# VectorE's dependent chains planned in parts, with VectorE's order left to the compiler

## The chip, the cores and the metric

The kernel runs on one core of one Trainium2 chip. The metric is device time in microseconds (us), the median over runs of one launch. "TensorE" and "PE" are the same engine, as are VectorE and DVE, ScalarE and ACT, GpSimd and POOL, SyncE and SP.

## What is computed

32 images of 128 channels and 56 x 56 points pass through two layers. Cut to what matters:

```python
# layer 0: convolution of signs
x = x + conv3x3(sign(groupnorm(x)), sign(w)) * Alpha
# layer 1: each point is a token of 128 channels
t = to_tokens(x)                                  # 3136 tokens per image
n = layernorm(t); q, k, v = n@Wq+bq, n@Wk+bk, n@Wv+bv
t = t + q * sum(k * v, over tokens)               # linear attention
n = layernorm(t)
p, e = top2(softmax(n @ router_w + router_b))     # 8 experts, 2 per token
t = t + sum_j p_j/sum(p) * (n @ expert_w[e_j] + expert_b[e_j])
out = from_tokens(t)
```

## The kernel before

The kernel is one long straight program, a software pipeline over the 32 images. An image's tokens stand in 25 chunks of up to 128 tokens (the last has 64), and these in 7 blocks of four. Each image goes through these steps, each of them a small Python function that emits the instructions of one engine: sums for the group norm (ScalarE), signs (ScalarE), convolution (`conv`, PE, 9 matmuls per 8 rows), adding it to x (`conv_add`, VectorE), transposing to tokens (`to_tokens`, PE), statistics of the first layer norm (`stats`, `var1`, `rstd1`, VectorE), the Gram matrix (`scaled`, `gram`), the product kv (`kv_1` to `kv_8`, taking turns on PE and VectorE), the bias of q (`bias`, VectorE), the projection (`project`, `project_out`, `project_add`), the second norm (`var2`, `rstd2`) and the routing (`route_1` to `route_5`, nearly all VectorE).

The experts are computed in two ways. The first 8 or 12 chunks of an image, and all chunks of the last four images, are "dense": gates are transposed, stored to memory, read back spread over all partitions (`spread`, a DMA to the tile `bc`), multiplied with the tokens (`gated`, VectorE, 128 x 1024) and put through all eight experts (`experts`, PE, tile `ff`). The other chunks of the first 28 images are "sorted": tokens are numbered by their pair of experts (`pair_of`, `places`, `row_numbers`, `row_scalars`), scattered to memory by GpSimd (tile `rows`), and, when a group of 8 or 4 images is complete, a list of tiles is made (`list_1`, `list_2`) and each tile of 128 rows goes through just two experts (`tile_load`, `tile_turn`, `tile_experts`, `tile_read`, `tile_sum`, `tile_out`). The results are gathered back (`result_rows`, `gather`).

What sets the order is a planner written in the kernel. `at(...)` (L444) records a step: its due time, engine, estimated work in us, function, the steps it comes after, and the buffers it takes and frees. `in_order` (L104) is a list scheduler: it keeps a clock for each engine, and of the steps that could start within `AHEAD` = 0.3 us of the earliest one, it takes that with the earliest due time (`urgency`, L133; a step that empties a PSUM bank counts as 7 us more urgent). A step that follows one of another engine is ready 0.5 or 0.8 us (`HOP`) after it. The list that results is emitted under `tc.manual_schedule(engines=IN_ORDER)` (L1684): the engines in `IN_ORDER` (L72: PE, VectorE, ScalarE) run exactly in the emitted order. The others, GpSimd and SyncE's DMA queue, are ordered by the compiler, which goes by the emitted order as a preference and by its own estimate of what is ready. In either case the order is fixed when the program starts, each engine takes its instructions strictly one after the other, and semaphores make it wait for its inputs.

A step of several VectorE instructions is one unit of this list; its instructions stand side by side on the engine, as in `rstd_of` (L464), where each needs the one before:

```python
for _ in range(NEWTON):
    nc.vector.tensor_mul(square, dst, dst)
    nc.vector.scalar_tensor_tensor(square, square, -0.5, var, ALU.mult, ALU.mult)
    nc.vector.scalar_tensor_tensor(dst, square, 1.5, dst, ALU.add, ALU.mult)
```

Lines that the prediction speaks of: L458 to L461 variance, L468 to L480 reciprocal root, L580 `conv_add`, L688 to L690 `kv_2`, L695 the matmul of `kv_3`, L736 `bias`, L862 to L893 routing, L1057 `gated`, L1075 `experts`, L1158 and L1159 `pair_of`, L1186 the first matmul of `places`, L1587 and L1592 `tile_sum` and `tile_out`.

Of the kernel before, what the change touches and what calls it, by code (L numbers as in the profile page):

```python
# [71 lines left out]
IN_ORDER = {mybir.EngineType.PE, mybir.EngineType.DVE, mybir.EngineType.Activation}  # L72
# [12 lines left out]
AHEAD = 0.3  # L85
# [7 lines left out]
class Step:  # L93
# [3 lines left out]
    def __init__(self, due, key, engine, work, do, args, after, take, free, delay, slack):  # L97
        self.due, self.key, self.engine, self.work = due, key, engine, work
        self.do, self.args, self.delay, self.slack = do, args, delay, slack
        self.after, self.take, self.free = after, take, free  # L100
        self.done = None


def in_order(steps):  # L104
# [28 lines left out]
    def urgency(s):  # L133

        return s.due - (EMPTIES if any(r in BANKS for r, _ in s.free) else 0.0)

    order = []
    while len(order) < len(steps):
        best = None
        for engine, pool in waiting.items():  # L140
# [9 lines left out]
            ((t, s) for t, s in starts if t <= first + AHEAD), key=lambda e: (urgency(e[1]), e[0])  # L150
# [7 lines left out]
        for f in followers.get(s.key, []):  # L158
            missing[f.key] -= 1

            same = f.engine == s.engine and (not s.delay or f.key[0] == s.key[0])
            f.ready = max(f.ready, clock[s.engine] if same else s.done + s.slack + HOP[f.engine])
            if not missing[f.key]:
                waiting.setdefault(f.engine, []).append(f)
# [4 lines left out]
def conv_attn_moe_kernel(  # L169
# [173 lines left out]
    def prepare():  # L343
# [3 lines left out]
        inv_c = spool.tile([1, C], F32, tag="kv", bufs=1, name="inv_c")  # L347
# [96 lines left out]
    def at(due, key, engine, work, do, *args, after=(), take=(), free=(), delay=0.0, slack=0.0):  # L444
        steps[key] = Step(due, key, engine, work, do, args, after, take, free, delay, slack)
# [6 lines left out]
    def var_of(stats, name):  # L452
# [3 lines left out]
        diff = spool.tile([C, n_ck], F32, tag="diff", name="diff")  # L456
        var = spool.tile([C, n_ck], F32, tag=name, name=name)
        nc.vector.tensor_sub(diff, mean_e, mean_o)  # L458
        nc.vector.scalar_tensor_tensor(diff, diff, 0.25, diff, ALU.mult, ALU.mult)
        nc.vector.scalar_tensor_tensor(var, m2_e, C * LN_EPS, m2_o, ALU.add, ALU.add)  # L460
        nc.vector.scalar_tensor_tensor(var, var, 1.0 / C, diff, ALU.mult, ALU.add)  # L461
        return var

    def rstd_of(var, dst):  # L464

        square = spool.tile([C, n_ck], F32, tag="square", bufs=1, name="square")
# [6 lines left out]
        )  # L473
        nc.vector.tensor_tensor(
            dst.bitcast(I32), guess.to_broadcast(shape), square.bitcast(I32), ALU.subtract
        )
        for _ in range(NEWTON):
            nc.vector.tensor_mul(square, dst, dst)
            nc.vector.scalar_tensor_tensor(square, square, -0.5, var, ALU.mult, ALU.mult)
            nc.vector.scalar_tensor_tensor(dst, square, 1.5, dst, ALU.add, ALU.mult)  # L480
# [8 lines left out]
    def plan_image(i: int):  # L489
# [57 lines left out]
        for j in range(GN_PARTS):  # L547
# [7 lines left out]
            s - 25, ("gn_total", i), "DVE", 0.09, gn_total,  # L555
# [4 lines left out]
            s - 23, ("gn_neg", i), "DVE", 0.08, gn_neg,  # L560
# [45 lines left out]
        def stats(g, st):  # L606
            for c in blocks[g]:
                n = rows_of(c)
                nc.vector.bn_stats(st[:n, c, :], d["tok"][:n, c, :C])  # L609

        def var1():
            d["var1"] = var_of(st1, "var1")
            d["r1"] = spool.tile([C, n_ck], F32, tag="r1", name=f"r1_{i}")

        def rstd1():
            rstd_of(d["var1"], d["r1"])
# [12 lines left out]
        for g in range(n_blk):  # L629
# [13 lines left out]
                due + 2, ("stats1", i, g), "DVE", 0.78 * share, stats, g, st1,  # L643
# [3 lines left out]
            s + 43, ("var1", i), "DVE", 0.45, var1,  # L647
            after=[("stats1", i, g) for g in range(n_blk)]
            + [("project_out", i - 2, 8), ("rstd1", i - 2)],
        )  # L650
        at(s + 44, ("rstd1", i), "DVE", 1.25, rstd1, after=[("var1", i)])
# [33 lines left out]
        def kv_2():  # L685
            tok_sum = d["g_sb"][:, C : C + 1]
            prod = spool.tile([C, C], F32, tag="prod", bufs=1, name=f"prod_{i}")
            nc.vector.scalar_tensor_tensor(prod, bv_bc, tok_sum, d["gv"], ALU.mult, ALU.add)  # L688
            nc.vector.tensor_mul(prod, prod, wk_sb)
            nc.vector.scalar_tensor_tensor(prod, wv_bk, tok_sum, prod, ALU.mult, ALU.add)  # L690
# [6 lines left out]
        def kv_4():  # L697

            kv = spool.tile([C, C], F32, tag="kv", bufs=1, name=f"kv_{i}")
            nc.vector.tensor_add(kv, n_bkbv, d["kv_ps"])  # L700
            nc.vector.tensor_mul(move[:, :C], wq_sb, kv)
# [8 lines left out]
        def kv_6():  # L710
# [3 lines left out]
            nc.vector.scalar_tensor_tensor(kr[:, 0, :], rw_sb, d["kvc"], one, ALU.mult, ALU.mult)  # L714
            nc.vector.scalar_tensor_tensor(
# [22 lines left out]
        for g in range(n_blk):  # L738
# [15 lines left out]
            ("PE", 0.25, kv_1), ("DVE", 0.73, kv_2), ("PE", 0.25, kv_3), ("DVE", 0.62, kv_4),  # L754
            ("PE", 0.25, kv_5), ("DVE", 0.28, kv_6), ("PE", 0.46, kv_7), ("ACT", 0.15, kv_8),
# [49 lines left out]
        def project_add(j):  # L805
# [10 lines left out]
            for c in cs:  # L816
                nc.vector.bn_stats(st2[:n, c, :], d["tok"][:n, c, :C])  # L817

        for j, cs in enumerate(q_groups):
# [12 lines left out]
                s + 87 + 3.5 * j, ("project_add", i, j), "DVE", 1.18 * share, project_add, j,  # L832
# [8 lines left out]
        def var2():  # L841
            d["var2"] = var_of(st2, "var2")
            d["r2"] = spool.tile([C, n_ck], F32, tag="r2", name=f"r2_{i}")

        def rstd2():
            rstd_of(d["var2"], d["r2"])
# [13 lines left out]
        def largest(vals, suffix):  # L860
            top, hot, best = narrow(f"top{suffix}"), wide(f"hot{suffix}"), narrow(f"best{suffix}")
            nc.vector.tensor_reduce(top, vals, AX.X, ALU.max)  # L862
            nc.vector.tensor_tensor(hot, vals, over_e(top), ALU.is_equal)
            nc.vector.tensor_tensor(hot, hot, over_c(rank), ALU.mult)
            nc.vector.tensor_reduce(best, hot, AX.X, ALU.max)
            nc.vector.tensor_tensor(hot, hot, over_e(best), ALU.is_equal)
            return top, hot, best

        def route_1():
            logit = wide("logit")  # L870
            nc.vector.tensor_tensor(logit, lgp, over_c(d["cq"]), ALU.add)
            nc.vector.tensor_tensor(logit, logit, over_e(d["r2"]), ALU.mult)
            nc.vector.tensor_tensor(logit, logit, over_c(rb_bc), ALU.add)
            d["logit"] = logit

        def route_2():
            d["top1"], d["hot1"], d["best1"] = largest(d["logit"], "1")
            rest = wide("rest")
            nc.vector.scalar_tensor_tensor(
                rest.rearrange("p c e -> p (c e)"),  # L880
                d["hot1"].rearrange("p c e -> p (c e)"),
                -BIG,
                d["logit"].rearrange("p c e -> p (c e)"),
                ALU.mult,
                ALU.add,
            )
            d["rest"] = rest

        def route_3():
            d["top2"], d["hot2"], d["best2"] = largest(d["rest"], "2")  # L890
# [7 lines left out]
        def route_5():  # L898
            gate1, gate2 = narrow("gate1"), narrow("gate2")
            nc.vector.tensor_tensor(gate1, d["ratio"], ones[:, :n_ck], ALU.add)  # L900
            nc.vector.reciprocal(gate1, gate1)
            nc.vector.tensor_mul(gate2, d["ratio"], gate1)
# [3 lines left out]
        def dense_gates():  # L906
# [7 lines left out]
            nc.vector.tensor_tensor(hot2, hot2, bc(d["gate2"]), ALU.mult)  # L914

            full = n // PER
            for lo, hi, per in ((0, full, PER), (full, n_db, n - full * PER)):
# [11 lines left out]
                nc.vector.tensor_tensor(plain, first, second, ALU.add)  # L929
                nc.vector.tensor_tensor(scaled_by, plain, r2, ALU.mult)  # L930
# [31 lines left out]
        def gate_parts():  # L962
# [5 lines left out]
            nc.vector.tensor_sub(parts[:, :, 1, :], p, parts[:, :, 0, :])  # L968
            nc.vector.tensor_sub(parts[:, :, 2, :], rem, parts[:, :, 1, :])

        def parts_store():
# [15 lines left out]
            s + 118, ("var2", i), "DVE", 0.45, var2,  # L987
            after=[("project_add", i, j) for j in range(last_q + 1)]
            + [("dense_gates", i - 2), ("row_scalars", i - 2)],
        )  # L990
        at(s + 119, ("rstd2", i), "DVE", 1.25, rstd2, after=[("var2", i)])
        at(s + 125, ("route_1", i), "DVE", 0.85, route_1, after=[("rstd2", i)] + routed)
        at(s + 126, ("route_2", i), "DVE", 1.7, route_2, after=[("route_1", i)])
        at(s + 128, ("route_3", i), "DVE", 1.53, route_3, after=[("route_2", i)])
        at(s + 130, ("route_4", i), "ACT", 0.14, route_4, after=[("route_3", i)])
        at(s + 131, ("route_5", i), "DVE", 0.43, route_5, after=[("route_4", i)])
        at(
            s + 135, ("dense_gates", i), "DVE", 0.8 * heavy, dense_gates,
# [16 lines left out]
            s + 138, ("gate_parts", i), "DVE", 0.65 * heavy, gate_parts,  # L1015
# [136 lines left out]
        def pair_of():  # L1152
# [6 lines left out]
            nc.vector.tensor_tensor(low, best1, best2, ALU.min)  # L1159

            nc.vector.scalar_tensor_tensor(pair, high, -3.0, high, ALU.add, ALU.mult)
            nc.vector.scalar_tensor_tensor(pair, pair, 0.5, low, ALU.mult, ALU.add)
            d["pair"] = pair

            mark = spool.tile([C, n_sort], F32, tag="mark", bufs=1, name=f"mark_{i}")
            nc.vector.tensor_add(mark, pair, no_row[:, most - n_sort :])
            shape = [C, n_sort, N_PAIR]
# [5 lines left out]
            )  # L1173
            with nc.allow_low_precision(reason="numbers up to four"):
# [42 lines left out]
        def row_numbers():  # L1217
# [3 lines left out]
            nc.vector.tensor_tensor(own, hot[:, :n_sort, :], d.pop("places")[:, :n_sort, :], ALU.mult)  # L1221
            nc.vector.tensor_reduce(place, own, AX.X, ALU.add)
            d["row_no"] = spool.tile([C, n_sort], U32, tag="row_no", bufs=4, name=f"row_no_{i}")
# [5 lines left out]
        def row_scalars():  # L1229
# [6 lines left out]
            swap, move_by, g = tmp("swap"), tmp("move_by"), tmp("g")  # L1236
# [498 lines left out]
```

## Time and profile before

| | |
|---|---|
| time, median of 3 runs | 2410.17 us (2406.23 to 2425.59) |
| the profiled execution's own time | 2401.99 us |
| its span, first to last instruction | 2400.3 us |
| granted TensorE clock, mean | 0.966 |
| PE busy | 2144.5 us (89%), 12074 instructions |
| weight loads (beside PE) | 1454.5 us (61%) |
| VectorE busy | 2097.1 us (87%), 6360 instructions |
| ScalarE busy | 1530.2 us (64%), 4883 instructions |
| GpSimd busy | 972.5 us (41%), 971 instructions |
| DMA | 448.56 MB, 187 GB/s in the mean |

An engine's busy time is the union of its instructions' intervals. On VectorE the interval of an instruction can overlap that of the next by some 80 ns, so the start of one to the start of the next is what an instruction costs. The profile's view of waits gives, for each line, the idle time of its engine just before it and who ended it; waits of 35 ns between two instructions of VectorE are not in it. VectorE's costliest groups: `gated` 449.1 us (384 instructions, 1177 ns each), the two lots of statistics 169.4 and 183.0 us (800 each), `conv_add` 151.2 us (224), `project_add`'s first addition 139.8 us (256 whole ones, 546 ns each).

### The profile page before, as it was taken

The numbers are of one execution on the slowest core, as the hardware profiler recorded it, in microseconds if no ns is written. First come the engines' busy times: TensorE is split into PE (matmuls) and PEld (weight loads), VectorE is DVE, ScalarE is ACT, GpSimd is POOL, SyncE is SP. The second block draws the span as 40 slices with busy tenths as digits, with TensorE's granted clock in tenths as the row PEclk, the third lists the DMA queues.
The fourth block names the chain that finished last, engine by engine and source line by source line (L and its number), as shares of the span: only waits on it lengthen the run. The fifth ranks groups of instructions, "written<-read, shape, count | busy, mean of one in ns | idle before, by whom it ended". The sixth has DMA issues, their size and how long they took to land. (4 is left out here: it accounts for less than half of the span.)

```text
span 2400.3 us, 45146 instructions
## 1 busy us (share of the span) xinstructions
PE 2144.5 (89%) x12074; PEld 1454.5 (61%) x12074; DVE 2097.1 (87%) x6360; ACT 1530.2 (64%) x4883; POOL 972.5 (41%) x971
## 2 busy tenths in 40 slices
PE   4889888888899999888999999898999888999889
PEld 2555555555676776555766766555676655766534
DVE  3899999999999999998889889999898777788875
ACT  3756666656788888566778876555687755674311
POOL 1033333333223234544445534554444444433554
PEclk9999999999999999999999999999999989999999
DMA  4044444445555655455667666666577656878688
GB/s 161 28 144 142 143 134 135 174 122 165 165 157 171 187 182 174 151 185 193 190 217 239 200 196 195 204 200 215 191 214 226 211 163 207 256 225 251 192 258 313
DMA packets 317740, 448.56 MB, mean 187 GB/s; under 512 B 61065, under 2 KB 223153, under 8 KB 317490
## 3 DMA queue, kind: packets, MB, share of 16 engines
q1 hardware_dynamic: 289090, 386.97, 51.4%
q0 software_dynamic: 27392, 55.17, 7.7%
q10 hardware_dynamic: 1008, 3.54, 0.4%
q8 instruction: 102, 1.67, 0.3%
q14 instruction: 148, 1.21, 0.2%
HBM read 319.51 MB, written 126.00 MB: 186 GB/s over the span
## 5 line engine op out<-in xcount | busy, mean ns | idle before, releaser
L1268 POOL DMA_INDIRECT rows<-tok,row_no x428 | 487.3, 1139 | 893.0 <-ACT tok L1262 400.0
L1075 PE MATMUL ff<-gated,ew_d 128*128 128x512 f32 (+1 forms) x1536 | 737.5, 608 | 78.8 <-DVE gated L1057 62.1
L1338 POOL DMA_INDIRECT back<-res,res_no x428 | 475.8, 1112 | 520.1 <-PE back_ps L1353 201.0
L1057 DVE TENSOR_TENSOR gated<-tt,bc 128x1024 f32<-128x1024 f32 x384 | 449.1, 1177 | 67.4 <-PE ff L1075 41.3
L1075 PEld LDWEIGHTS ff<-gated,ew_d 128*128 128x128 f32 x1536 | 277.0, 196 | 324.4 <-issue 220.6
L569 PE MATMUL cv<-xs,w_bin 128*128 128x448 bf16 x2016 | 438.6, 365 | 11.8 <-ACT xs L535 5.8
L1575 ACT ACTIVATE v<-to,t_in 128x128 f32<-128x128 f32 x528 | 251.1, 476 | 119.1 <-PE to L1557 47.6
L569 PEld LDWEIGHTS <-w_bin 128*128 128x128 bf16 x2016 | 201.0, 100 | 188.0 <-issue 43.4
L798 ACT ACTIVATE qs<-q,r 128x136 f32<-128x136 f32 (+1 forms) x800 | 246.4, 401 | 88.4 <-PE q L784 44.9
L1557 PEld LDWEIGHTS to<-ew_s,turned 128*128 128x128 f32 x2112 | 258.4, 193 | 48.5 <-issue 23.7
L1557 PE MATMUL to<-ew_s,turned 128*128 x2112 | 270.4, 278 | 17.8 <-ACT tok L602 6.4
L660 ACT ACTIVATE y<-tok,r 128x128 f32<-128x128 f32 (+1 forms) x800 | 253.6, 403 | 39.9 <-DVE r L480 21.8
L784 PE MATMUL q<-move,x 128*128 128x144 f32 (+1 forms) x1600 | 239.2, 295 | 10.0 <-ACT qs L802 3.6
L784 PEld LDWEIGHTS q<-move,x 128*128 128x128 f32 (+1 forms) x1600 | 213.7, 193 | 40.8 <-issue 17.5
L669 PEld LDWEIGHTS gram<-y 128*128 128x128 f32 (+1 forms) x1600 | 200.5, 191 | 45.3 <-issue 27.3
L669 PE MATMUL gram<-y 128*128 128x129 f32 (+1 forms) x1600 | 213.1, 278 | 2.2 <-ACT y L660 1.9
L1582 ACT ACTIVATE w<-to,t_in 128x128 f32<-128x128 f32 x528 | 204.0, 386 | 0.0
L580 DVE SCALAR_TENSOR_TENSOR x<-cv,alpha_col,x 128x448 f32<-128x448 f32 x224 | 151.2, 675 | 47.6 <-PE cv L569 29.8
L602 ACT COPY tok<-xt 128x512 f32<-128x512 f32 (+1 forms) x224 | 118.4, 564 | 115.9 <-PE xt L596 72.9
L609 DVE BATCH_NORM_STATS2 st<-tok 128x6 f32<-128x128 f32 (+1 forms) x800 | 169.4, 277 | 21.7 <-ACT tok L602 17.5
L817 DVE BATCH_NORM_STATS2 st<-tok 128x6 f32<-128x128 f32 (+1 forms) x800 | 183.0, 282 | 0.0
L1262 ACT ACTIVATE tok<-tok,a 128x128 f32<-128x128 f32 (+1 forms) x428 | 168.5, 428 | 9.5 <-DVE a L1250 9.3
(216 smaller groups left out, 2902.9 us busy)
## 6 DMA issues: line engine op xcount, KB each, us to landing
bc<-gp SPq DMA_DIRECT2D x368, 512.0 KB
x<-in_x_dram SPq DMA_DIRECT2D x64, 784.0 KB
t_in<-rows SPq DMA_DIRECT2D x528, 66.0 KB
res<-v SPq DMA_DIRECT2D x132, 256.0 KB
out_dram<-o SPq DMA_DIRECT2D x100, 256.0 KB
out_dram<-tt SPq DMA_DIRECT2D x92, 256.0 KB
rows<-zeros SPq DMA_DIRECT2D x116, 66.0 KB
rows<-tok,row_no POOLq DMA_INDIRECT x428
```

Of the source, the lines that this page charges most:

```text
L569: nc.tensor.matmul(cv, lhsT=w_bin[:, t, :], rhs=xs[:, b * ROWS + dy : b * ROWS + dy + ROWS, dx : dx + width], start=(t == 0), stop=(t == T ...
L660: nc.scalar.mul(y[:n, j, :C], d["tok"][:n, c, :C], d["r1"][:n, c : c + 1])
L669: nc.tensor.matmul(d["gram"], lhsT=y[:n, j, :C], rhs=y[:n, j, :], start=(c == 0), stop=(c == n_ck - 1),)
L784: nc.tensor.matmul(p[:n, k, :], lhsT=d["x"][:, c * C : c * C + n], rhs=move, start=True, stop=True,)
L798: nc.scalar.mul(qs[:n, k, : C + N_EXP], p[:n, k, : C + N_EXP], d["r1"][:n, c : c + 1])
L1057: nc.vector.tensor_tensor(g[:, :, :n], d["tt", b][:, :n].unsqueeze(1).to_broadcast([C, 2, n]), d.pop(("bc", b, k))[:, :, :n], ALU.mult,)
L1075: nc.tensor.matmul(d["ff", b][:, :n], lhsT=ew_d[:, e * C : (e + 1) * C], rhs=g[:, j, :n], start=False, stop=(e == N_EXP - 1),)
L1268: dma = nc.gpsimd.indirect_dma_start(out=groups[group]["rows"], out_offset=bass.IndirectOffsetOnAxis(ap=d["row_no"][:n, c - n_dense : c - ...
L1338: dma = nc.gpsimd.indirect_dma_start(out=d["back", c][:n, :], out_offset=None, in_=groups[group]["res"][: quads_of(group) * WIDE, :], in_o ...
L1557: nc.tensor.matmul(p[:, k, j, :], lhsT=t[:, n * C : (n + 1) * C], rhs=ew_s[:, bass.ds(d["cols", q][j][n], C)], start=True, stop=True,)
L1575: nc.scalar.activation(d["v", q][:, n, :], p[:, k, 0, :], AF.Identity, bias=row[:, C + 2 : C + 3], scale=row[:, C : C + 1],)
L1582: nc.scalar.mul(d["w", q][:, n, :], p[:, k, 1, :], row[:, C + 1 : C + 2])
```

## The change

The functions that emit a dependent chain on VectorE become generators that `yield` between the parts. `at` takes a list of work figures for such a step (a tuple for a step that is only divisible, such as statistics) and records one step per part, each after the one before, so that the planner can put other VectorE steps between two parts. A part of a list is ready `LAG` = 0.12 us after the part before has left the engine, and counts as 3 us more urgent (`CHAINS`). `AHEAD` becomes one figure per engine, 0.05 us for VectorE and 0.3 as before for the others. Some work figures change with it (`rstd1`, 1.25 us before, is eleven parts of 0.10 us). Temporaries that two chains shared get buffers of their own (`diff1`, `diff2`, `square1`, `square2`, `own2`, `by`, `h`), `kv` moves into the buffer of `prod`, `rest` into that of `logit`. In `row_scalars` and `list_2` independent instructions are grouped so that fewer neighbours depend on each other; `list_4` copies only the used part of the list. And VectorE is taken out of `IN_ORDER`: the compiler orders its instructions, as it does GpSimd's and SyncE's; PE and ScalarE keep the emitted order. The diff moves no instruction to another engine.

```diff
-IN_ORDER = {mybir.EngineType.PE, mybir.EngineType.DVE, mybir.EngineType.Activation}
+IN_ORDER = {mybir.EngineType.PE, mybir.EngineType.Activation}
-AHEAD = 0.3
+AHEAD = dict(PE=0.3, DVE=0.05, ACT=0.3, POOL=0.3, SP=0.3)
+CHAINS = 3.0
+LAG = 0.12
     def urgency(s):
-        return s.due - (EMPTIES if any(r in BANKS for r, _ in s.free) else 0.0)
+        empties = EMPTIES if any(r in BANKS for r, _ in s.free) else 0.0
+        return s.due - empties - (CHAINS if s.lag else 0.0)
...
-            ((t, s) for t, s in starts if t <= first + AHEAD), key=lambda e: (urgency(e[1]), e[0])
+            ((t, s) for t, s in starts if t <= first + AHEAD[s.engine]),
+            key=lambda e: (urgency(e[1]), e[0]),
...
-            f.ready = max(f.ready, clock[s.engine] if same else s.done + s.slack + HOP[f.engine])
+            f.ready = max(
+                f.ready, clock[s.engine] + s.lag if same else s.done + s.slack + HOP[f.engine]
+            )
...
     def at(due, key, engine, work, do, *args, after=(), take=(), free=(), delay=0.0, slack=0.0):
-        steps[key] = Step(due, key, engine, work, do, args, after, take, free, delay, slack)
+        if isinstance(work, float):
+            steps[key] = Step(due, key, engine, work, do, args, after, take, free, delay, slack, 0.0)
+            return
+        running = []
+        def go_on():
+            if not running:
+                running.append(do(*args))
+            next(running[0], None)
+        lag = LAG if isinstance(work, list) else 0.0
+        for j, w in enumerate(work):
+            last = j == len(work) - 1
+            part = key if last else (*key, "part", j)
+            steps[part] = Step(
+                due, part, engine, w, go_on, (), [(*key, "part", j - 1)] if j else after,
+                [] if j else take, free if last else [], delay if last else 0.0, slack, lag,
+            )
...
-    def rstd_of(var, dst):
-        square = spool.tile([C, n_ck], F32, tag="square", bufs=1, name="square")
+    def rstd_of(var, dst, name):
+        square = spool.tile([C, n_ck], F32, tag=f"square{name}", bufs=1, name="square")
...
         for _ in range(NEWTON):
+            yield
             nc.vector.tensor_mul(square, dst, dst)
+            yield
             nc.vector.scalar_tensor_tensor(square, square, -0.5, var, ALU.mult, ALU.mult)
+            yield
             nc.vector.scalar_tensor_tensor(dst, square, 1.5, dst, ALU.add, ALU.mult)
...
-        at(s + 44, ("rstd1", i), "DVE", 1.25, rstd1, after=[("var1", i)])
+        at(s + 44, ("rstd1", i), "DVE", [0.10] * (2 + 3 * NEWTON), rstd1, after=[("var1", i)])
...
-            ("PE", 0.25, kv_1), ("DVE", 0.73, kv_2), ("PE", 0.25, kv_3), ("DVE", 0.62, kv_4),
-            ("PE", 0.25, kv_5), ("DVE", 0.28, kv_6), ("PE", 0.46, kv_7), ("ACT", 0.15, kv_8),
+            ("PE", 0.25, kv_1), ("DVE", [0.26, 0.21, 0.27], kv_2), ("PE", 0.25, kv_3), ("DVE", [0.19, 0.41], kv_4),
+            ("PE", 0.25, kv_5), ("DVE", [0.14, 0.14], kv_6), ("PE", 0.46, kv_7), ("ACT", 0.15, kv_8),
...
-        at(s + 126, ("route_2", i), "DVE", 1.7, route_2, after=[("route_1", i)])
-        at(s + 128, ("route_3", i), "DVE", 1.53, route_3, after=[("route_2", i)])
+        at(s + 126, ("route_2", i), "DVE", [0.28] * 6, route_2, after=[("route_1", i)])
+        at(s + 128, ("route_3", i), "DVE", [0.28] * 4 + [0.38], route_3, after=[("route_2", i)])
...
-                s + 87 + 3.5 * j, ("project_add", i, j), "DVE", 1.18 * share, project_add, j,
+                s + 87 + 3.5 * j, ("project_add", i, j), "DVE", (0.58 * share,) + (0.19,) * len(cs), project_add, j,
```

The same pattern (a list of work figures and a `yield` between dependent instructions) is applied to `var_of`, `kv_2`, `kv_4`, `kv_6`, `route_1`, `route_5`, `dense_gates`, `gate_parts`, `pair_of`, `row_numbers`, `row_scalars`, `result_rows`, `list_1` and `list_2`.

## The prediction

> **What bounds the kernel now.** I read the page's busy shares first (PE 89%, VectorE 87%: neither bounds it alone), then the busy time by stretch, then the waits of VectorE and of PE inside the stretch that looked fullest, and last VectorE's timeline for what its instructions cost. Busy time by stretch: span, then PE, PE's weight load, VectorE (DVE), ScalarE (ACT), GpSimd (POOL), each with its count, then the granted clock and the DMA share.
>
> ```profile
> 100.00:600.00 500.00, 435.13 (x2379) 281.82 (x2380) 478.17 (x1632) 312.42 (x1042) 170.07 (x148) 0.96 0.43 139
> 600.00:1100.00 500.00, 460.18 (x2812) 326.70 (x2811) 473.34 (x1513) 374.74 (x1217) 181.93 (x160) 0.98 0.56 172
> 1100.00:1600.00 500.00, 466.91 (x2781) 329.17 (x2781) 451.00 (x1347) 359.61 (x1144) 241.37 (x217) 0.99 0.66 207
> ```
>
> From 100 to 1100 us VectorE shows 951.5 us busy in 1000, PE 895.3. The view of waits for VectorE in that stretch (total, times, longest) begins with this line, and all its waits over 0.1 us sum to 9.7 us, 22 of them:
>
> ```profile
> DVE x L580 <- PE cv L569: 4.3, 5, 1.6
> ```
>
> So VectorE never runs dry there: the 39 us missing from its busy time are gaps of some 35 ns between instructions. PE does wait, and on VectorE:
>
> ```profile
> PE ff L1075 <- DVE gated L1057: 35.1, 31, 2.4
> PE kv_ps L695 <- DVE prod L690: 17.5, 12, 2.2
> PE xt L596 <- DVE x L580: 11.1, 7, 4.2
> PE places L1186 <- DVE hot L1168: 9.1, 9, 3.6
> ```
>
> By releaser, PE's waits over 0.1 us from 100 to 1100 us are 85.8 us on VectorE, 6.8 on ScalarE and 12.1 on nothing the profile shows. From 1100 to 2300 us they are 52.4 on VectorE, 22.2 on ScalarE, 5.5 on DMA and 20.7 on nothing shown, and VectorE itself waits 132 us there, 108 times, so 1.22 us each. The kernel is VectorE's in its first half and shared in its second.
>
> VectorE's timeline (start, duration, line) shows what a chain costs:
>
> ```profile
> 1212.59 0.20 DVE L458 TENSOR_TENSOR diff<-st 128x25 f32<-128x25 f32 x1
> 1212.82 0.19 DVE L459 SCALAR_TENSOR_TENSOR diff<-diff 128x25 f32<-128x25 f32 x1
> 1212.93 0.19 DVE L460 SCALAR_TENSOR_TENSOR var<-st 128x25 f32<-128x25 f32 x1
> 1213.16 0.19 DVE L461 SCALAR_TENSOR_TENSOR var<-var,diff 128x25 f32<-128x25 f32 x1
> ...
> 1222.97 0.18 DVE L893 TENSOR_TENSOR ratio<-top,top 128x25 f32<-128x25 f32 x1
> 1223.06 0.17 DVE L1158 TENSOR_TENSOR high<-best,best 128x13 f32<-128x13 f32 x1
> 1223.14 0.17 DVE L1159 TENSOR_TENSOR low<-best,best 128x13 f32<-128x13 f32 x1
> ```
>
> L459 needs L458's result and starts 0.23 us after it; L460 needs nothing of L459 and starts 0.11 us after that, inside its 0.19 us; L461 needs L460 and is 0.23 us off again. L1158 and L1159, independent, follow at 0.09 and 0.08. So a dependent follower costs 0.22 to 0.23 us of VectorE, an independent one about 0.10. For the 200-wide routing instructions it is 0.40 against 0.29 us (L866 at 1222.68 to L893). A link of a chain wastes 0.11 to 0.12 us; I take 0.115.
>
> **The parts.** *Chains cut in parts.* Links per image by the code: two norms (variance and reciprocal root) 13 each, routing 14, the gates 2, 3 and 1, the kv products 4, and for a sorted image pair_of 5, row_numbers 2, row_scalars 7, result_rows 4: 68, and 50 without the last four. 28 x 68 + 4 x 50 = 2104. The trace agrees: 2208 of VectorE's 6360 instructions start 20 to 60 ns after their predecessor's end; less the 132 tile_sum/tile_out pairs, which the change does not cut, 2076. At 0.115 us that is 239 us of VectorE time, if something independent stands in every gap.
>
> From 100 to 1100 us there are 1128 - 40 = 1088 links: 125 us. VectorE's need falls from 990 to 865 us, below PE's 895. PE then sets the pace, at the best share it has where VectorE is not full: 466.9 of 500, 93.4% (1100 to 1600 us). 895.3 / 0.934 = 958: **-42 us**. A quarter of the links hidden (32 us) would reach nearly that, so it doesn't hang on every link.
>
> From 1100 to 2300 us VectorE has room, and shorter chains help only where PE waited on VectorE: 52 us; I take half, **-26**. Both ends: 0 and -52. The first 100 us (loading and preparing) and the last 100 (transfers and single matmuls) keep their times: 0.
>
> *A rule against this.* By "VectorE: DVE Perf Modes", section "The DRAIN you can't avoid", the next VectorE instruction does not start until the pipe is empty, whether it depends or not, so its advice on chained operations is to cut their number and not to expect more. By it the two terms above would be 0 and the forecast 2402. The rows above speak otherwise for these shapes: L1158 starts 0.09 us into L893's 0.18.
>
> *Latency of one chain.* Cutting lets other work in between. A gated instruction (1.14 us) between two parts of kv_2 holds up PE, whose queue is fixed: PE's waits on prod are 29 us in all. Ends: -29 if the parts are preferred (the new urgency term of 3 us does that), +73 if a gated goes into both gaps of every image (32 x 2 x 1.14). I take 0, as nearest to the present.
>
> *row_scalars and list_2 regrouped, own tags for diff, square, own, by:* the same instructions (11 and 11), fewer waits on shared buffers, all inside VectorE's queue: 0, cover as above. *kv in prod's buffer:* kv_4 waits for kv_3 to have read prod, but it reads kv_3's result anyway: 0. *The biases* (L736, 132 us of VectorE with the short form) stay on VectorE; the diff does not move them: 0.
>
> *Planner's figures.* It now gives rstd 11 x 0.10 + 10 x 0.12 = 2.3 us instead of 1.25; the timeline shows 11 x 0.22 = 2.4. PE's and ScalarE's emitted orders come from better figures. No row prices that; left in the range.
>
> *VectorE ordered by the compiler.* It adds no instruction, but any instruction whose input is late on the chip holds all behind it: gated (PE's ff), conv adds (the next transposes), scalars for ScalarE. No trace of before shows VectorE so. The nearest rows: SyncE and GpSimd are ordered by the compiler already. Laying the planner's list beside the trace, 762 of the 935 SyncE issues that can be matched stand exactly at the planner's place and none is over 5 off; of GpSimd's 856, 614, none over 3 off. So I expect the emitted order with neighbours swapped. Each wrong swap on the path costs about the mean wait, 1.22 us. Below: one fewer per image, -39. Above: three more, 32 x 3 x 1.22 = +117. I take **+15** (12 of them), near the close agreement of the two queues.
>
> Sum against the profiled execution (2401.99 us, span 2400.3): 2402 - 42 - 26 + 15 = 2349. That run lies 8 us under the shown median of 2410, so on the median's scale 2357.
>
> **Rivals.** *Slower: head-of-line waits on VectorE.* From 100 to 1100 us it now has 22 waits; there a wait is lost time outright. With three misplaced instructions per image: 2402 - 68 + 117 = 2451, about 2460. It decides from 68 / 1.22 = 56 waits, 1.7 per image. For it: transfers and PE's clock (0.91 to 1.00 between stretches of 100 us) vary in ways no fixed order foresees, and VectorE's dependences cross engines far more than SyncE's. Against it: the two queues' agreement, and VectorE's backlog in the first half, where the next instruction is usually ready.
>
> *Larger gain.* All of PE's waits on VectorE outside fill and tail go: 138 us, 2402 - 138 + 8 = 2272. For it: VectorE falls to about 87% of the first half. Against: something is late next; ScalarE already has 22 us of PE's waits in the second half.
>
> *No change: PE is the wall, or the parts end up side by side.* If the compiler emits a chain's parts back to back, or PE's fixed order only moves its waits, VectorE's saving turns into idle: about 2400. Against: the emitted list has the parts apart already.
>
> **Numbers.** Forecast case (2325 to 2385) 0.43, larger gain 0.14, no change 0.15, slower 0.28. The likeliest is 2357. The range, 2285 to 2465, takes in most of the larger gain and the slower case at three waits per image. About 1% (2386 to 2434) is what a measurement of this kernel can tell from no change: faster 0.57, within 0.15, slower 0.28.
>
> **What would show it.** VectorE's instructions that start 20 to 60 ns after their predecessor's end fall from 2208 to under 1000, and its busy time by 100 us or more. From 100 to 1100 us PE's share rises from 89.5% to 93% and its waits on gated fall by half. Wrong: the links stay; or VectorE's waits in that stretch, 9.7 us, grow past 60, mostly on PE or transfers, with a PE share no better; or PE's waits on prod grow past 29 us.

## The result and the profile after

The changed kernel takes 2475.35 us in the median (2471.34 to 2481.45, 4 runs) beside 2408.83 us before: a ratio of 1.0263, with a 95% interval from 1.0212 to 1.0315. It is slower, against the forecast of 2357 us, and outside the range of 2285 to 2465. Its profiled execution took 2475.12 us, its span is 2473.4 us, and the granted TensorE clock in the mean 0.944 (0.966 before).

VectorE did get its time back: busy 1982.5 us instead of 2097.1, and 903 instructions start 20 to 60 ns after their predecessor's end instead of 2198 (the 2208 of the prediction also take in ten more gaps under 100 ns). VectorE's timeline (start, duration, line; profile after) shows the parts of one chain with other work between them:

```profile
304.46 0.18 DVE L488 SCALAR_TENSOR_TENSOR diff<-diff 128x25 f32<-128x25 f32 x1
304.56 0.68 DVE L1134 TENSOR_TENSOR tt<-tt,ff 128x512 f32<-128x512 f32 x1
305.15 0.18 DVE L490 SCALAR_TENSOR_TENSOR var<-var,diff 128x25 f32<-128x25 f32 x1
305.25 0.36 DVE L915 TENSOR_TENSOR logit<-lgp,cq 128x200 f32<-128x200 f32 x1
305.52 0.18 DVE L496 TENSOR_TENSOR square<-var,one_i 128x25 int32<-128x25 int32 x1
305.62 0.18 DVE L1298 TENSOR_TENSOR mean<-st 128x17 f32<-128x17 f32 x1
```

L488, L490 and L496 are a chain; with a neighbour in each gap the next instruction starts 0.06 to 0.09 us before the end of the one in front, nowhere 0.03 us after it. (L1298 belongs to `row_scalars`.) Not every link is hidden: the same chain's next seven instructions, from 305.74 us on, stand side by side again.

Busy time by stretch (profile after; columns as before: span, PE, PE's weight load, VectorE, ScalarE, GpSimd, clock, DMA share, GB/s):

```profile
100.00:600.00 500.00, 457.61 (x2596) 305.92 (x2595) 480.06 (x1762) 342.65 (x1136) 202.21 (x153) 0.96 0.47 151
600.00:1100.00 500.00, 457.60 (x2767) 325.64 (x2766) 442.38 (x1507) 367.93 (x1198) 200.42 (x170) 0.95 0.57 174
1100.00:1600.00 500.00, 424.77 (x2525) 301.27 (x2523) 379.62 (x1173) 324.21 (x1030) 236.82 (x191) 0.92 0.60 182
```

From 100 to 600 us PE has 457.6 us of work where it had 435.1: the gain is there. From 600 to 1100 us it grows no further (457.6 beside 460.2), and from 1100 to 1600 us PE falls from 466.9 to 424.8 us and VectorE from 451 to 380: both engines stand idle more, so neither is the bound. Counting finished matmuls says the same: what the kernel before has done at 1100 us, the changed kernel has done 34 us earlier; what it has done at 1300 us, 5 us later. VectorE's waits from 100 to 1100 us (total, times, longest; profile after):

```profile
DVE res_no L1395 <- DMA back<-res,res_no: 9.5, 1, 9.5
DVE x L612 <- PE cv L601: 9.5, 1, 9.5
```

and from 1100 to 2300 us:

```profile
DVE res_no L1395 <- DMA back<-res,res_no: 131.7, 15, 17.9
DVE v L1672 <- ACT w L1667: 34.2, 25, 3.2
```

All waits of VectorE over 0.1 us grew from 222.7 to 455.2 us over the span, and 141.2 us of the 232 are one line, L1395: the last instruction of `result_rows`, which writes the row numbers `res_no` that GpSimd's gathers read. There are four buffers of `res_no`; image i's can be written only when image i-4's gathers have landed. Before, that line (L1333) stood idle for 4.5 us in all, never over 0.3; its largest entry in the view of waits (profile before) is

```profile
DVE res_no L1333 <- DVE by L1332: 1.8, 8, 0.2
```

One such wait on VectorE's timeline, with its idle time and releaser in brackets:

```profile
1186.50 0.69 DVE L1134 TENSOR_TENSOR tt<-tt,ff 128x512 f32<-128x512 f32 x1 [2.43 <-PE ff L1123]
1204.83 0.18 DVE L1395 TENSOR_TENSOR res_no<-by,place 128x17 uint32<-128x17 f32 x1 [17.64 <-DMA back<-res,res_no]
1205.04 0.65 DVE L1389 TENSOR_REDUCE by<-own 128x17 f32<-128x476 f32 x1
```

and PE's timeline around it:

```profile
1199.62 1.05 PE L1642 MATMUL to<-ew_s,turned 128*128 x8
1211.78 2.08 PE L1642 MATMUL to<-ew_s,turned 128*128 x8 [11.10 <-DVE x L612]
1214.08 2.40 PE L1123 MATMUL ff<-gated,ew_d 128*128 128x512 f32 x4
```

VectorE stands still for 17.6 us over row numbers of image 7 that no gather needs yet (the plan has the gathers of one image after those of the other). PE lives on its queue until 1200.7, then waits 11.1 us for a `conv_add` (L612, at 1211.05 us) that stands 15 places behind L1395: to 1204.8 us VectorE waits, after that it works off what has piled up. And PE comes back slowly: a group of eight like matmuls takes 2.08 us after the pause and 1.05 before it. Busy time by stretch shows the granted clock (third from the end):

```profile
1187.00:1201.00 14.00, 13.68 (x101) 10.73 (x99) 0.19 (x1) 11.94 (x37) 5.88 (x7) 1.00 0.32 97
1201.00:1209.00 8.00, 0.00 (x0) 0.00 (x0) 4.13 (x11) 1.15 (x4) 6.17 (x7) 0.74 0.19 51
1209.00:1220.00 11.00, 7.76 (x29) 5.06 (x30) 10.55 (x36) 3.29 (x10) 2.96 (x1) 0.72 0.96 309
```

Why L1395 stands there can be read from the order in which VectorE's instructions ran. With VectorE in the emitted order (e1 below), 3898 instructions run before this one of image 7 (images are numbered from 0); in the changed kernel 3626 do. Over the 28 sorted images the compiler moved the five instructions of `result_rows` up by medians of 190 (the last) to 494 (the first) places, 1843 at most; an image has some 200 VectorE instructions. 5830 of all 6360 instructions are within 20 places. `result_rows` reads only `pair`, `place` and the tile list, which are there that early. That it comes after the gathers of image i-3 is written in the planner's list of steps, and the compiler, which sees data and buffers only, is not bound by it.

### The profile page after: what moved, and what is told of

The parts are those of the page before. It is cut to its first block, busy times and chain, and to the rows that moved or that the text cites. A ratio compares the mean times of both kernels' runs of the same rounds, so it can differ in the third digit from the quotient of the medians.

```text
span 2473.4 us, 45194 instructions
## 1 busy us (share of the span) xinstructions
PE 2148.2 (87%) x12074; PEld 1467.2 (59%) x12074; DVE 1982.5 (80%) x6360; ACT 1528.3 (62%) x4883; POOL 1041.7 (42%) x971
## 3 DMA queue, kind: packets, MB, share of 16 engines
q14 instruction: 150, 1.22, 0.2%
## 4 chain that ended last, share of the span: by engine, by line
PE 54%; DVE 20%; DMA 11%; issue 7%; ACT 4%; POOL 2%; SPq 1%; another core or an unknown queue 1%; DVEq 0%; ACTq 0%; POOLq 0%
PE ff L1123 19%; PE cv L601 10%; PE to L1642 6%; PE gram L703 5%; PE q L822 4%; DVE gated L1105 3%; DMA rows<-tok,row_no 2%; DVE st L641 2%; DMA back<-res,res_no 2%; DVE tok L774 2%; DMA t_in<-rows 2%; PE xt L628 2%; DVE st L856 2%; PE turn L1624 2%; DVE tok L848 1%
## 5 line engine op out<-in xcount | busy, mean ns | idle before, releaser
L1325 POOL DMA_INDIRECT rows<-tok,row_no x428 | 538.4, 1258 | 826.0 <-ACT tok L1319 328.3
L1123 PE MATMUL ff<-gated,ew_d 128*128 128x512 f32 (+1 forms) x1536 | 745.3, 616 | 116.0 <-DVE gated L1105 81.3
L1400 POOL DMA_INDIRECT back<-res,res_no x428 | 493.9, 1154 | 588.4 <-PE back_ps L1415 293.6
L1123 PEld LDWEIGHTS ff<-gated,ew_d 128*128 128x128 f32 x1536 | 284.0, 200 | 369.3 <-issue 250.7
L601 PE MATMUL cv<-xs,w_bin 128*128 128x448 bf16 x2016 | 426.2, 359 | 11.8 <-issue 6.3
L641 DVE BATCH_NORM_STATS2 st<-tok 128x6 f32<-128x128 f32 (+1 forms) x800 | 179.7, 277 | 18.3 <-ACT tok L634 14.2
L856 DVE BATCH_NORM_STATS2 st<-tok 128x6 f32<-128x128 f32 (+1 forms) x800 | 192.7, 278 | 0.0
L612 DVE SCALAR_TENSOR_TENSOR x<-cv,alpha_col,x 128x448 f32<-128x448 f32 x224 | 151.2, 675 | 50.5 <-PE cv L601 34.2
```

The lines of the kernel that those rows point to most:

```text
L601: nc.tensor.matmul(cv, lhsT=w_bin[:, t, :], rhs=xs[:, b * ROWS + dy : b * ROWS + dy + ROWS, dx : dx + width], start=(t == 0), stop=(t == T ...
L1123: nc.tensor.matmul(d["ff", b][:, :n], lhsT=ew_d[:, e * C : (e + 1) * C], rhs=g[:, j, :n], start=False, stop=(e == N_EXP - 1),)
L1325: dma = nc.gpsimd.indirect_dma_start(out=groups[group]["rows"], out_offset=bass.IndirectOffsetOnAxis(ap=d["row_no"][:n, c - n_dense : c - ...
L1400: dma = nc.gpsimd.indirect_dma_start(out=d["back", c][:n, :], out_offset=None, in_=groups[group]["res"][: quads_of(group) * WIDE, :], in_o ...
```

## The experiments

Three theories were set against each other: that the loss is `result_rows` run early, that it is many small swaps, and that the parts themselves cost. The runs e1 to e4, e5 to e7, e8 to e11 and e12 to e14 each share a chip and runs of the kernel before. That kernel took 2400 us on the first chip, and 2345, 2344 and 2345 on the others; differences in us are taken within a chip only. The profile before was taken with the result, not with these runs; its 2402 us are near the 2400 of e1's chip.

**e1, e11, e14: VectorE in the emitted order.**

```diff
-IN_ORDER = {mybir.EngineType.PE, mybir.EngineType.Activation}
+IN_ORDER = {mybir.EngineType.PE, mybir.EngineType.DVE, mybir.EngineType.Activation}
```

> The changed kernel with VectorE put back among the engines that keep the emitted order; nothing else differs. Theory 'early result_rows' (the compiler runs result_rows hundreds of instructions early, and its last instruction then stands at the head of VectorE's queue until a gather frees a res_no buffer): the 141 us of VectorE waits at that line vanish and the chains' gain shows, 2330 to 2370 us. Rival 'many small swaps': the same here, 2330 to 2370. Rival 'the parts themselves cost' (urgent chains are stretched by what is put between their parts): still 2440 or more.

> e1_hand_order again, beside the other three: both theories expect a ratio of 0.955 to 0.975, the lowest of the four.

> e11_hand_again once more, as the neighbour of e12 on its chip: ratio to the kernel before 0.955 to 0.965, PE's waits on gated 30 to 36 us.

2304.89 us beside 2399.9: ratio 0.9599 (0.9546 to 0.9652); again 2244.86 beside 2344.07, 0.9581 (0.9547 to 0.9616), and 2239.91 beside 2344.9, 0.9555 (0.9536 to 0.9573). The parts do not cost; with their figures and buffers they gain 4%, more than forecast, and e1 is below the range given. The rival "the parts cost" is out. This version beats both kernels.

**e2, e9, e13: only result_rows in the planner's place.** VectorE is still ordered by the compiler; `front` is the VectorE instruction emitted last, and `issue_after` queues behind it without a wait.

```diff
         for step in in_order(steps):
-            step.do(*step.args)
+            if step.key[0] == "result_rows" and front is not None:
+                with tc.issue_after(front):
+                    step.do(*step.args)
+            else:
+                step.do(*step.args)
...
```

> The changed kernel, VectorE still ordered by the compiler, but each result_rows instruction is queued behind the VectorE instruction that the planner puts before it. Theory 'early result_rows': waits at res_no fall from 141 us to under 15, time 2350 to 2400 us. Rival 'many small swaps': they are all still there, 2440 or more. Rival 'the parts cost': 2440 or more.

> e2_result_rows_in_place again, beside e8 and e10: theory 'early result_rows': 100 to 125 us below e8, ratio 0.98 to 0.99. Rival 'many small swaps': less than 50 us below e8.

> e9_result_rows_again once more, as the neighbour of e12 on its chip: ratio to the kernel before 0.97 to 0.985, PE's waits on gated 50 to 60 us.

2360.47 us, ratio 0.9848 (0.9790 to 0.9905); on the next chip 2277.76, 0.9727 (0.9690 to 0.9764); on the third 2278.07, 0.9714 (0.9692 to 0.9736). Waits for a gather at L1395 are 0.9 us or less in all in the profiles of e2 and e9; VectorE's wait in e9:

```profile
DVE res_no L1395 <- DMA back<-res,res_no: 0.2, 1, 0.2
```

One step, put back, turns a loss of 3.7% (e8, below) into a gain of 2.7%. The gain is larger than e9's expectation: 151 us below e8 instead of 100 to 125. The one step does not come back alone, though: of the 6220 VectorE instructions outside `result_rows`, 400 are over 20 places from the planner's in the changed kernel, 170 in e2. Whether the wait or these others made the difference, e3 decides.

**e8: the changed kernel on the chip of e9 to e11.**

> The changed kernel again, unchanged, beside the next three on one chip, since the kernel before took 2400 us on the chip of e1 to e4 and 2345 on that of e5 to e7. Theory 'early result_rows': ratio to the kernel before 1.02 to 1.03, waits at res_no 120 to 160 us. Rival 'the loss hangs on the chip': ratio under 1.01.

2429.12 us, ratio 1.0365 (1.0325 to 1.0405), a larger loss than the 1.02 to 1.03 expected. VectorE's wait in e8:

```profile
DVE res_no L1395 <- DMA back<-res,res_no: 158.3, 17, 18.4
```

So on one chip: changed kernel 2429, `result_rows` put back (e9) 2278, emitted order (e11) 2245. Putting `result_rows` back is worth 151 of the 184 us. The three kernels' busy time by stretch shows where; e8:

```profile
100.00:1100.00 1000.00, 926.60 (x5526) 644.35 (x5525) 938.85 (x3318) 732.88 (x2410) 414.75 (x332) 0.97 0.53 168
1100.00:1700.00 600.00, 513.72 (x2940) 356.11 (x2938) 475.12 (x1498) 370.32 (x1181) 288.81 (x237) 0.93 0.59 184
```

e9:

```profile
100.00:1100.00 1000.00, 936.17 (x5569) 651.18 (x5567) 944.86 (x3330) 737.69 (x2421) 418.40 (x336) 0.97 0.53 169
1100.00:1700.00 600.00, 564.89 (x3335) 398.24 (x3334) 527.35 (x1675) 419.27 (x1342) 328.29 (x270) 0.97 0.68 212
```

e11:

```profile
100.00:1100.00 1000.00, 950.34 (x5714) 665.93 (x5713) 964.11 (x3380) 755.14 (x2476) 395.37 (x344) 0.97 0.55 174
1100.00:1700.00 600.00, 568.78 (x3331) 396.77 (x3330) 527.99 (x1696) 422.33 (x1345) 321.00 (x274) 0.97 0.69 216
```

Up to 1100 us the three are close: 926.6, 936.2 and 950.3 us of PE work done in the same time. From 1100 us on, where the gathers run, e8 does 514 us of PE work in 600 and the others 565 and 569.

**e3: 16 buffers of res_no.** The compiler still runs `result_rows` early, but nothing has to be waited for.

```diff
-            d["res_no"] = spool.tile([C, n_sort], U32, tag="res_no", bufs=4, name=f"res_no_{i}")
+            d["res_no"] = spool.tile([C, n_sort], U32, tag="res_no", bufs=16, name=f"res_no_{i}")
-            own = spool.tile(shape, F32, tag="own2", bufs=1, name=f"own2_{i}")
+            own = spool.tile(shape, F32, tag="own", bufs=1, name=f"own2_{i}")
```

> The changed kernel with 16 buffers for res_no instead of 4 (and the temporary own2 back in the buffer of own, to make room); the compiler still runs result_rows early, some 140 instructions in the median. Theory 'early result_rows', where the harm is the wait for a buffer and not the place: waits at res_no under 15 us, time 2350 to 2410 us. Rival 'the place itself harms' (result_rows' work displaces urgent work): 2430 or more without such waits. Rival 'many small swaps': 2440 or more.

2363.43 us, ratio 0.9844 (0.9808 to 0.9880), the same as e2 on that chip, and no wait over 0.1 us at L1395. The second change of its diff, made for room, also holds `result_rows` back somewhat (compare e5), but its last instruction still stands 141 places early in the median, and of the instructions outside `result_rows` 667 are over 20 places from the planner's, more than in the changed kernel (400). So early places as such, of this step and of others, do not make the loss that e2 undoes; the wait at the head of the queue does.

**e5: two shared buffers restored.** `own2` and `by` go back into the buffers of `own` and `high`, as before the change.

```diff
-            own = spool.tile(shape, F32, tag="own2", bufs=1, name=f"own2_{i}")
-            by = spool.tile([C, n_sort], F32, tag="by", bufs=1, name=f"by_{i}")
+            own = spool.tile(shape, F32, tag="own", bufs=1, name=f"own2_{i}")
+            by = spool.tile([C, n_sort], F32, tag="high", bufs=1, name=f"by_{i}")
```

> The changed kernel with only two buffers undone: result_rows' temporaries own2 and by go back into the buffers of own and high, as before; VectorE still ordered by the compiler, res_no still 4 buffers. In the built order its last instruction then stands 74 places ahead of the planner's in the median (193 at most) instead of 189 (1535). Theory 'own buffers let result_rows run away': waits at res_no fall from 141 us to 10 to 40, time 2360 to 2410 us. Rival 'the compiler's order with parts does it, whatever the buffers': waits at res_no over 100 us, 2450 or more.

2333.09 us beside 2344.58: ratio 0.9950 (0.9932 to 0.9969), against e8's 1.0365. VectorE's waits in e5:

```profile
DVE res_no L1395 <- DMA back<-res,res_no: 43.6, 9, 11.0
```

The wait came out slightly over the 10 to 40 us expected, the ratio as the theory has it (0.9950 x 2400 = 2388; the 2360 to 2410 us were meant for the chip of e1). The last instruction of `result_rows` stands 81 places early in the median of this profile. The two buffers, shared with `row_numbers` and `pair_of` of other images, had kept `result_rows` near its place; taking them apart let it go. That is some 4% of the time, for about 2 KB per partition (own2 is 17 x 28 floats).

**e4: the kernel before, VectorE ordered by the compiler.** Only the line of e1's diff differs, in the other kernel and the other direction.

> The kernel before with VectorE taken out of the emitted order and nothing else changed. Theory 'early result_rows': they move up by some 60 to 180 instructions in the median here, so waits at res_no of 40 to 120 us and 2430 to 2490 us. Rival 'the parts cost': the compiler's order is harmless by itself, 2400 to 2420 us.

2392.97 us (10 runs), ratio 0.9965 (0.9928 to 1.0002). That is below both ranges and nearer the rival's: the compiler's order costs nothing in sum here. That the parts cost, which the rival concluded from this, is out by e1. The theory's 40 to 120 us of waits did not come either. VectorE's waits in e4:

```profile
DVE v L1587 <- ACT w L1582: 70.4, 36, 9.3
DVE res_no L1333 <- DMA back<-res,res_no: 18.7, 5, 9.2
```

With the shared buffers `result_rows`' last instruction moved up by 59 places in the median, and waited 18.7 us. And the compiler put other work into the chains by itself: 983 instructions start 20 to 60 ns behind their predecessor's end instead of 2198, VectorE's busy time is 1990 us. It gave that back in waits, 374 us instead of 223.

**e7: emitted order, but the planner doesn't know of the chains.** On e1:

```diff
-CHAINS = 3.0
-LAG = 0.12
+CHAINS = 0.0
+LAG = 0.0
```

> As e1_hand_order, but the planner doesn't know of the chains: LAG 0 and CHAINS 0, parts and buffers kept. Theory 'a dependent neighbour costs 0.115 us, and the planner's lag is what takes it away': instructions that start 20 to 60 ns behind their predecessor's end rise from 882 to 1400 or more, and the time to 2340 to 2390 us. Rival 'better work figures and buffers make the gain': 2300 to 2320 us.

2316.17 us, ratio 0.9863 (0.9839 to 0.9888), where the emitted order with lag has 0.9581 and 0.9555 on chips with the same kernel-before time. Links (instructions that start 20 to 60 ns behind their predecessor's end) rose to 1781, as expected. Taken as they stand, the 2316 us lie in the rival's range; both ranges had been meant for the chip of e1, where the ratio would give 0.9863 x 2400 = 2367, in the theory's. By the ratios, `LAG` and `CHAINS` together carry about two thirds of the gain (4.2 - 1.4 = 2.8 of 4.2%). The rest is left for better work figures, divisible steps, buffers and regrouping; no run separates these.

**e6, e10: three more steps in the planner's place.** On e2's loop:

```diff
-            if step.key[0] == "result_rows" and front is not None:
+            if step.key[0] in ("result_rows", "tile_sum", "row_numbers", "gn_total") and front is not None:
```

> As e2_result_rows_in_place, and the same for tile_sum, row_numbers and gn_total: each queued behind the VectorE instruction that the planner puts before it. Theory 'a few steps whose input the compiler expects too early make up the rest' (VectorE waits on ScalarE's w 44 us, count_h 24, junk 25): those three fall under 40 us together and the time comes to 2315 to 2345 us. Rival 'many small swaps, no step in particular': 2350 to 2370 us, with the waits moved to other lines.

> e6_more_in_place again, beside e9 and e11. Theory 'a few steps whose input the compiler expects too early': 20 to 45 us below e9 and within 25 us of e11. Rival 'many small swaps': within 10 us of e9.

2295.12 us on one chip (0.9788, 0.9766 to 0.9810), 2292.43 on the chip of e9 (0.9772, 0.9734 to 0.9811), there 15 us above e9. The waits on `w`, `count_h` and `junk` fell to 38 us together, as expected, but others took their place (on `tok`, `ff`, `qs`). The steps with VectorE's longest waits were not what held the rest of the loss; this expectation failed. The rival's "within 10 us of e9" failed too, by 5 us on the slow side.

**e12: nothing may pass gated.** On e2's loop; `passed` is the last `gated` emitted:

```diff
-            if step.key[0] == "result_rows" and front is not None:
-                with tc.issue_after(front):
+            behind = front if step.key[0] == "result_rows" else passed
+            if step.engine == "DVE" and behind is not None:
+                with tc.issue_after(behind):
```

> As e2/e9 (result_rows in the planner's place), and no VectorE instruction may be moved ahead of a gated instruction that the planner puts before it; gated itself may still move up. In e9's order a tenth of the 384 gated instructions stand 16 places or more later than the planner has them, here none. Theory 'gated passed by others is the rest of the compiler's loss': PE's waits on gated fall from 57 to about 35 us and the time to within 12 us of e14, that is 20 us or more below e13. Rival 'many small swaps': within 10 us of e13.

2258.38 us, ratio 0.9636 (0.9612 to 0.9659), between its neighbours e13 (2278.07) and e14 (2239.91). PE's waits (e13, then e12, then e14):

```profile
PE ff L1123 <- DVE gated L1105: 56.9, 38, 3.7
```

```profile
PE ff L1123 <- DVE gated L1105: 26.8, 14, 3.7
```

```profile
PE ff L1123 <- DVE gated L1105: 35.0, 19, 3.7
```

PE's wait on `gated` went below that of the emitted order, and 20 of the 38 us came back, but not the 26 that "within 12 us of e14" needs. So about half of the remainder goes with keeping other VectorE work behind `gated`; some 18 us stay unexplained, and "many small swaps" is left open for them. On the chip of e1 the remainder is larger (e2 is 56 us above e1) and was not divided.

## Why the prediction was wrong

*What bounds the kernel: right.* VectorE was the bound of the first half. With its chains hidden and the order kept, PE does 939 to 950 us of work from 100 to 1100 us instead of 895 (e1, e11); 934 was forecast.

*The chains' gain: right in kind, too small.* Terms of -42 and -26 us, 68 together, gave 2.8%; e1 measures 95 us, 4.0%. The first term is the one that fell short. What the kernel before has done at 1100 us, counted in finished matmuls, e1 has done at 1028: 72 us earlier, and nearly every larger kind of matmul taken alone gives 67 to 75. From there to the end e1 gains 28 us, near the -26. The forecast held PE's work in that stretch at 895 us; e1 needs 875 for the same number of matmuls, and over the whole span 2117 instead of 2145. Why PE is busy for less time is open: the mean granted clock is 0.966 in both profiles. (The forecast's count of links that stay, 132 pairs with 40 in the first half, was high: 109 of these pairs show the gap, 28 of them in the first half. That moves neither term.)

*The compiler's order: the step that failed.* The forecast had "+15 (12 of them), near the close agreement of the two queues". It measured +184 us on one chip (e8 against e11), 151 of them undone by putting one step back (e9). Both the number and the price were wrong. The size of a misplacement: 1.22 us was VectorE's mean wait in an order that had been planned around those waits; a misplaced `res_no` waited 158.3 / 17 = 9.3 us, since what it waits for stands in a queue of its own: in the 17.6 us shown above GpSimd issued eight gathers and two scatters. And the nearness: the two queues stand within 5 places of the planner, but VectorE's `result_rows` stood up to 1843 off. A reason that fits, not tested: SyncE's and GpSimd's steps are tied to data that come late (a landed tile, a finished row), and their nearness says little of a step whose order stands only in the planner's `after`.

*Own buffers: a second failed step.* "The same instructions, fewer waits on shared buffers, all inside VectorE's queue: 0." With the order kept that may hold; with the compiler's order the shared buffers were the ties, and e5 shows the ratio 1.0365 against 0.9950 for two of them.

*The rival "head-of-line waits on VectorE"* had the side and nearly the time (2460), with the wrong size and place: it had 96 swaps of 1.22 us each; there are 16 or 17 waits of some 9 us each, of one step, all but one after 1100 us. That its time came near is luck: a gain of the chains put too small and a loss put too small partly cancel.

*The signs.* The links and VectorE's busy time fell as forecast in the changed kernel itself. PE's share from 100 to 1100 us came to 91.5%, and PE's waits on `gated` there only fell from 35.1 to 32.2 us; with the order kept (e1) they are 93.9% and 18.2 us. The sign of being wrong did not come true as written: VectorE's waits in that stretch grew to 62.3 us, just past 60, but PE's share was better, not "no better", and on e8's chip they are 41 us. The loss stood later, where no sign was set.

*The rule on chained operations.* The prediction read "VectorE: DVE Perf Modes", section "The DRAIN you can't avoid", as a rule that would make the chain terms 0. The runs decide against that for these shapes: 2198 links to 882, VectorE's busy time 2097 to 1980 us (e1), and the kernel 4% faster. The prediction left out that the section itself goes on to say "A next op that is not held starts earlier"; the independent neighbours in the rows above do start earlier, as that sentence allows.

## What to carry to other kernels

An order that stands only in a plan, and not in data or buffers, can be lost when another scheduler takes over: look for steps whose inputs are ready early and whose output buffer comes free late, for their last instruction can come to stand at the head of a queue. Giving temporaries buffers of their own removes ties that may have been what kept a step in place. A dependent neighbour on VectorE costs 0.11 to 0.12 us in the rows before the change (128x25 and 128x200), about as much as a small independent instruction takes (0.10), so putting independent work between is worth about as much as removing one. The compiler's order does part of that without any parts (e4: 2198 links to 983).

## What the runs showed of the hardware beyond that

A pause of PE is paid twice. e8 and e9 have the same matmuls; PE's busy time is 2135 us in e8 and 2099 in e9, the mean granted clock 0.946 and 0.971. That is 36 of the 151 us between them, if the clock is all that differs in it (it need not be: before and e1 differ by 27 us of PE's busy time at one mean clock). The timeline above shows it: after 11 us idle a group of eight like matmuls takes 2.08 us instead of 1.05. "TensorE: Matmul & The Clock Gate", section "Part 1: The HAM clock gate", says that PE runs at half its clock after an idle window and until it has been busy for a while; the row agrees.

The same program differs by chip. The kernel before took 2400 us on one and 2344 to 2345 on three others, e1 and e11 (one program) 2305 and 2245, at clocks of 0.966 and 0.972 in their profiles. PE's waits that no releaser explains are 36.5 us from 100 to 2300 us in e1 and under 0.3 in e11. What they are stays open.
